# Graph attention and a GCN layer: transposing x1's rows in square blocks by VectorE and DMA, with three more products in the seven-product form

## The chip, the cores and the metric

One core of one Trainium2 chip runs the whole kernel. The metric is the device time of one execution in microseconds. Where a profile is quoted, PE is TensorE (PEld its weight loads), DVE is VectorE, ACT is ScalarE, POOL is GpSimd and SP is SyncE, which here only issues DMAs. L740 is line 740 of the kernel before.

## What is computed

All arrays are f32. x is 4096 x 512, adj is 4096 x 4096, the attention weights are 512 x 512, W1 is 512 x 128 and W2 is 128 x 512.

```python
q, k, v = x @ Wq.T + bq, x @ Wk.T + bk, x @ Wv.T + bv
a = q @ k.T / sqrt(512) + adj + adj
x1 = layernorm(x + softmax(a) @ v)
h = relu(adj @ (x1 @ W1) + b1)
out = layernorm(x1 + adj @ (h @ W2) + b2)
```

## The kernel before, in words

Rows are handled in 8 groups g of 512 (each of 4 row blocks r of 128). The scores are not made from q and k. The kernel forms M from Wq and Wk (`psm`, L856), then for each group u = M^T x^T (`psu`), and scores come from x^T and u alone; the softmax weights multiply x itself (`p`, L576), and only then comes the product with Wv.

Most large products use a seven-product form (Winograd's variant of Strassen's): the two operands are cut into quarters, seven half-size products are made instead of eight, and sums and differences of quarters go to other engines. `OPERANDS` names the operands of each product and `ORDER` their order. S1 to S4 are sums of quarters of the left operand (`form_s`), T1 to T4 of the right one. A transposing product by the identity matrix is used where a tile must be turned.

**Stages.** Time is cut into units of 7 steps; 16 units make a stage. In stage g, each step holds two products of the scores of group g (`qk`, L436), and beside them come items of a work list: the products `p` of group g-1 with x, and, at the start of the stage, the rows of group g-2 (`row_items`, L754). Items have a cost in microseconds; the loop at the end pops them at an even rate over the stage, so their order in the list is the order on every engine. `between(n)`, written `w(n)` in the list, takes n items of `p`; an item of cost 0 issues no matmul. So the rows of groups 0 to 5 lie in stages 2 to 7; those of group 6 lie beside `p` of group 7 in a stage 8 that has no scores, and those of group 7 beside the first product of the second layer. Stage 0 has no rows; its list holds the products of u for later groups.

**The rows of a group** (`row_items`): the product with Wv, for groups 0 to 5 (`FAST_V`) in the seven-product form (`rows_out_fast`, L659, 28 matmuls of 128x256), for groups 6 and 7 in the plain one (`rows_out`, L645, 16 matmuls of 128x512); the layer norm (`norm`: `rows_norm`, L726, on ACT); `add_b2` (L729), which adds b2 on POOL and stores the row block; `project` (L736), which turns a row block of x1 by four 128x128 transposes on PE (`x1ps`, L740) and copies them out by ACT into `x1t` (L742); and `project2` (L745), four matmuls of x1t with W1 (`tps`, L749). x1 stands in `xr`, one buffer, and x1t in one buffer that it shares with the scratch tile s3 of `rows_out_fast`.

**u.** Groups 0 and 1 use the plain form (`u_products`, L254, 16 matmuls of 128x512 each, L262); u of group 0 is computed before the first scores, and u of group 1 beside units 0 to 2. Groups 2 to 7 use the seven-product form (`u_fast`, L194, 28 matmuls of 128x256 each, L234) beside units 3 to 15. Its operands T1 to T4 of M come from `m_sums` and `m_t3`. u of groups 1 to 7 is stored to DRAM (`store_u`) and loaded back in its stage.

**DMA.** SP issues in program order the loads of x for `p` (`xn`, L506 and L510, three phases ahead; a phase is one operand of one block of 2 or 4 tile pairs), those of the score operands (`sa`, L342 and L347, five products ahead) and others. An instruction that waits holds up all that SP has behind it. ACT stores the score constants of a group by `store_c` (`c_d`, L417): 512 separate values of 4 bytes to DRAM.

Of the kernel before, what the change touches and what calls it, by code (L numbers as in the profile page):

```python
# [18 lines left out]
P = 128  # L19
# [5 lines left out]
def tile_graph_attention_then_gcn(  # L25
# [79 lines left out]

    c_d = [dram.tile([1, W], F32, name=f"c_d{g}") for g in range(NG)]
    u_d = [dram.tile([P, 7, 2, HW], F32, name=f"u_d{g}") for g in range(NG)]
    s_d = {
# [44 lines left out]

    FAST_V = range(NG - 2)
    QUARTER = {1: (0, 0), 2: (0, 0), 6: (1, 0), 7: (1, 1), 5: (1, 1), 4: (1, 0), 3: (0, 1)}
# [9 lines left out]
    def new_uo(b, what):  # L165

        u = UO.setdefault(b, {})
        if what in (B11, B12):
            u[what] = uop.tile([P, 2, HW], F32, tag="b1", name=f"b1_{b}_{what}", bufs=3)
        else:  # L170
            u["all"] = uop.tile([P, 5, 2, HW], F32, tag="ut", name=f"uo{b}")
            u.update({k: u["all"][:, k - 1] for k in range(1, 6)})

    def store_u(b, what):
        if what in (B11, T4):
            nc.gpsimd.dma_start(u_d[b][:, what], UO[b][what])
        else:
            nc.gpsimd.dma_start(u_d[b][:, 1:6], UO[b]["all"])

    def m_sums():  # L180

        m = m_t.rearrange("p (f c) (h o) -> p f h c o", f=2, h=2)
        for k, v in ((B11, m[:, 0, 0]), (T3, m[:, 0, 1]), (B21, m[:, 1, 0]), (B22, m[:, 1, 1])):
            MV[k] = v
        MV[T1] = t_sb[:, 28:32, :].rearrange("p (c a) b -> p c (a b)", c=2)
        MV[T2], MV[T4] = (ms_t[:, n] for n in range(2))
        for out_, a, b_ in ((T1, T3, B11), (T2, B22, T1), (T4, B21, T2)):
            nc.gpsimd.tensor_tensor(MV[out_], MV[a], MV[b_], ALU.subtract)

    def m_t3():  # L190

        nc.vector.tensor_tensor(MV[T3], MV[B22], MV[T3], ALU.subtract)

    def u_fast(b):  # L194
# [4 lines left out]
        def read(k):  # L199
            ps = X["X" if k in (1, 6, 5, 3) else "Y"].rearrange("p (o i) -> p o i", o=2)  # L200
            if k == 1:
                new_uo(b, B11)
            if k == 6:
                new_uo(b, B12)
            if k == 7:
                new_uo(b, "all")
            to = UO[b][{1: B11, 2: B11, 6: B12, 4: B12, 7: B22, 5: B22, 3: B21}[k]]
# [9 lines left out]
            if k == 4:  # L217
                for out_, a, b_ in ((T1, B12, B11), (T2, B22, T1), (T3, B22, B12)):
                    nc.gpsimd.tensor_tensor(u[out_], u[a], u[b_], ALU.subtract)
                store_u(b, B11)  # L220
            if k == 3:
                store_u(b, "all")
                owing.append(lambda: last(b))

        def last(b):
            nc.vector.tensor_tensor(UO[b][T4], UO[b][B21], UO[b][T2], ALU.subtract)
            store_u(b, T4)

# [23 lines left out]
        return [one(k, j) for k in ORDER for j in range(2)]  # L252

    def u_products(b):  # L254

        ps = {}

        def one(o, c):
            def go():
                if c == 0:  # L260
                    ps[o] = bank("o", f"psu{b}_{o}", 4)
                nc.tensor.matmul(  # L262
                    ps[o], m_t[:, c, ts(o, P)], XTS[b][:, c, :], start=c == 0, stop=c == ND - 1
                )
                if c == ND - 1:
                    if o == 0:
                        if b:
                            for what in (B11, B12, "all"):
                                new_uo(b, what)
                        else:  # L270
                            for k in ORDER:
                                new_operand(0, k)
                    pair = (B11, B12) if o < 2 else (B21, B22)
                    for h in range(2):
                        nc.scalar.activation(
                            (UO[b][pair[h]] if b else UT[0, pair[h]])[:, o % 2, :],
                            ps[o][:, ts(h, HW)],
                            AF.Identity,
                            bias=ub_t[:, o : o + 1],
                            scale=HALF_SCALE,  # L280
                        )
                    if o == ND - 1:
                        if b:
                            combine_u(nc.gpsimd, UO[b])
                            for what in (B11, "all", T4):
                                store_u(b, what)
                        else:
                            combine_u(nc.vector, {k: UT[0, k] for k in range(7)})

            return go  # L290

        return [one(o, c) for o in range(ND) for c in range(ND)]

    def combine_u(eng, ut):
        for out_, a, b_ in ((T1, B12, B11), (T2, B22, T1), (T3, B22, B12), (T4, B21, T2)):
            eng.tensor_tensor(ut[out_], ut[a], ut[b_], ALU.subtract)

# [361 lines left out]
    def rows_out_fast(g, k, j):  # L659
# [5 lines left out]
        tt = nc.vector.tensor_tensor  # L665

        def read(k):
            ps = T["VX" if k in (1, 6, 5, 3) else "VY"].rearrange("p (j o) -> p j o", j=2)
            h, i = QUARTER[k]
            to = XR[g][:, 2 * h : 2 * h + 2, ts(i, HW)]  # L670
            tt(to, ps, to, ALU.add)
# [18 lines left out]
        if (k, j) == (1, 0):  # L690
            read_px()
            T["s3"] = rowp.tile([P, 2, HW], F32, tag="x1t", name=f"s3_{g}")
            tt(T["s3"], a11, a21, ALU.subtract)
            tt(a21, a21, a22, ALU.add)
        if j == 0 and k in (1, 2, 7):
# [16 lines left out]
        if j == 0 and n:  # L712
            read(ORDER[n - 1])
            if k == 2:
                tt(a11, a21, a11, ALU.subtract)
            if k == 6:
                tt(a12, a12, a11, ALU.subtract)
            if k == 3:
                stats(2)
# [16 lines left out]
    def project(g, r):  # L736
# [5 lines left out]
        nc.scalar.copy(x1t.rearrange("p c i -> p (c i)"), ps)  # L742
        T["x1t", g, r] = x1t

    def project2(g, r):  # L745
# [8 lines left out]
    def row_items(g, between):  # L754
# [3 lines left out]
        def item(us, f, *args):  # L758
            return us, lambda: f(*args)
# [15 lines left out]

        w = between
        if g in FAST_V:
            return [
                *(item(0.86, rows_out_fast, g, k, j) for k in ORDER for j in range(2)),
                *w(1), item(0, rows_last, g), *norm(2), *norm(3), *w(2), *pro(2), *w(2), *pro(3),  # L780
                *w(1), *norm(0), *w(1), *pro2(2), *norm(1), *w(2), *pro(0), *w(2), *pro2(3), *w(2),
# [11 lines left out]
    with tc.tile_pool(name="wqk", bufs=1) as wp:  # L793
# [46 lines left out]

        for w_t, w_n, name, b_t, b_r in (
            (wq_t, wq_n, "bk", bk_t, bk_r), (wk_t, wk_n, "bq", bq_t, bq_r)
        ):
            in_every_row(name, b_t, b_r)
            for o in range(ND):
                ps = bank("o", f"psw{o}", 4)
                for c in range(ND):
                    nc.tensor.transpose(ps[:, ts(c, P)], w_t[:, c, ts(o, P)], ident)
                evict(o, w_n[:, o, :], ps)
        times(wq_t, bk_r, g_c)  # L850
        times(wk_t, bq_r, ub_t)

        for a in range(ND):
            ps = bank("o", f"psm{a}", 4)
            for o in range(ND):
                nc.tensor.matmul(  # L856
                    ps, wq_n[:, o, ts(a, P)], wk_n[:, o, :], start=o == 0, stop=o == ND - 1
                )
            evict(a, m_t[:, a, :], ps)
            if a == 1:  # L860
                in_every_row("g", g_c, g_t)
                times(bq_r.unsqueeze(1), bk_r, c0_t)
                for r in range(PER):
                    row_parts(r, rows0[:, r, :])
                add_c0(0)

    SLOTS = 12

    adjp = ctx.enter_context(tc.tile_pool(name="adjp", bufs=SLOTS))
    first = u_products(0)  # L870
    for f in first[:ND]:
        f()
    row_consts(0)
    begin_scores(0, 0)
    add_scores(0, 0)
    for f in form_s(0):
        f()
    for f in first[ND:]:
        f()

# [15 lines left out]

    work = {}
    work[0] = 3, [(0.86, f) for f in u_products(1)]
    work[3] = 13, [(0.86, f) for g in range(2, NG) for f in u_fast(g)] + [(0, lambda: owing.pop()())] * 2
    at(1, 0, m_sums)  # L900
    at(3, 0, m_t3)
    for g in range(2, NG):
# [216 lines left out]
    for g in range(NG):  # L1119
# [8 lines left out]
        for q in range(NP):  # L1128
            d, j = divmod(q, 2)
            if (g or d) and j == 0:  # L1130
                early = 2 + (g == 1 and d < 2)
                at(s0 + q - early, 4, begin_scores, g, d)
                at(s0 + q - early, 5, add_scores, g, d)
            for h in range(2):
# [262 lines left out]
```

## Time and profile before

| | |
|---|---|
| median of 3 runs | 2304.07 us (2303.71 to 2310.33) |
| profiled execution, its own time | 2308.84 us |
| its span in the trace | 2307.1 us |
| granted TensorE clock, mean | 0.998 |
| PE busy | 2276.3 us, 99% |
| DVE busy | 1617.0 us, 70% |
| POOL busy | 1018.7 us, 44% |
| ACT busy | 399.8 us, 17% |
| DMA queue q1 (SP), share of 16 engines | 52.3% |
| DMA queue q0 (POOL), share of 16 engines | 20.7% |

The span is the time from the first to the last instruction in the trace. Matmuls are pipelined, so what one costs is read from the distance between the starts of neighbours. An f32 matmul stands as two records in the trace, a transpose as one.

### The profile page before, as it was taken

What the parts mean: (1) busy time and instruction counts of PE and PEld (TensorE: products, weight loads), DVE (VectorE), ACT (ScalarE), POOL (GpSimd) and SP (SyncE); (2) the same over time, 40 slices, a digit from 0 to 9 for tenths busy, and PEclk for the clock granted to TensorE, in tenths of its full rate; (3) what the DMA queues carried; (4) which work ended last, traced back from release to release, by engine and by line L of the source; (5) the groups of instructions that cost most, each with busy time, mean ns of one, the idle gap of its engine ahead of it and who ended that gap; (6) DMA issues with size and microseconds to landing.
All of it is one profiled execution on the core that took longest, in us unless ns stands there. A gap on an engine that the chain in (4) does not pass through costs nothing.

```text
span 2307.1 us, 28475 instructions
## 1 busy us (share of the span) xinstructions
PE 2276.3 (99%) x10672; PEld 1750.6 (76%) x10672; DVE 1617.0 (70%) x2276; ACT 399.8 (17%) x438; POOL 1018.7 (44%) x1009
## 2 busy tenths in 40 slices
PE   9999999999999999999999999999999999999998
PEld 5888788888888888888888888888876743333456
DVE  4676776687667756765776687568657877888864
ACT  2212211131122112111311121122102000000012
POOL 3565654185327424731653274237429830001043
PEclk9999999999999999999999999999999999999999
DMA  6999878667857684777578586947754468899996
GB/s 177 273 284 309 233 215 230 193 174 215 246 135 218 189 246 114 215 213 215 151 221 232 145 218 193 259 117 210 196 191 155 155 237 321 332 347 375 352 383 218
DMA packets 282711, 525.14 MB, mean 228 GB/s; under 512 B 23184, under 2 KB 130448, under 8 KB 281680
## 3 DMA queue, kind: packets, MB, share of 16 engines
q1 hardware_dynamic: 229040, 406.12, 52.3%
q0 software_dynamic: 43296, 105.39, 20.7%
q10 hardware_dynamic: 10240, 11.82, 1.7%
q8 instruction: 85, 1.39, 0.2%
q14 instruction: 50, 0.41, 0.0%
HBM read 475.27 MB, written 46.41 MB: 226 GB/s over the span
## 4 chain that ended last, share of the span: by engine, by line
PE 92%; DVE 4%; POOL 2%; DMA 1%; issue 1%; ACT 0%; SPq 0%; POOLq 0%; DVEq 0%; ACTq 0%
PE p L576 32%; PE X L436 18%; PE b L1041 15%; PE Y L436 14%; PE v L703 3%; PE acce L1342 2%; PE psu L234 2%; PE ops L1296 1%; PE tps L749 1%; PE psu L262 1%; PE x L651 1%; PE x1ps L740 1%; DVE s L449 1%; PE psm L856 1%; DMA u_d<-uo 1%
## 5 line engine op out<-in xcount | busy, mean ns | idle before, releaser
L576 PE MATMUL p<-s,xn 128*128 128x256 f32 x3584 | 895.6, 380 | 7.0 <-DVE s L531 2.6
L576 PEld LDWEIGHTS p<-s,xn 128*128 128x128 f32 x3584 | 677.1, 190 | 111.0 <-DVE s L531 5.6
L436 PE MATMUL X<-ut,sa 128*128 128x256 f32 x1984 | 513.4, 381 | 1.7 <-DVE s L449 1.7
L492 POOL TENSOR_TENSOR lacc<-lacc,s 128x512 f32<-128x512 f32 x240 | 344.1, 1434 | 203.2 <-ACT s L483 192.3
L436 PEld LDWEIGHTS X<-ut,sa 128*128 128x128 f32 x1984 | 370.1, 190 | 64.2 <-DVE s L449 15.3
L449 DVE TENSOR_TENSOR s<-X,s 128x512 f32<-128x512 f32 x256 | 176.3, 689 | 278.6 <-PE X L436 278.2
L436 PE MATMUL Y<-ut,sa 128*128 128x256 f32 x1408 | 361.6, 380 | 0.2 <-DVE s L449 0.2
L436 PEld LDWEIGHTS Y<-ut,sa 128*128 128x128 f32 x1408 | 266.8, 190 | 37.7 <-issue 1.4
L483 ACT ACTIVATE s<-s 128x1024 f32<-128x1024 f32 x128 | 135.3, 1057 | 790.3 <-DVE s L479 790.3
L458 DVE TENSOR_TENSOR macc<-macc,s 128x512 f32<-128x512 f32 x240 | 258.1, 1075 | 1.2
L449 DVE TENSOR_TENSOR s<-Y,s 128x512 f32<-128x512 f32 x192 | 131.9, 687 | 157.0 <-PE Y L436 155.7
L479 DVE TENSOR_TENSOR s<-s,mb 128x512 f32<-128x512 f32 x256 | 231.2, 913 | 2.4 <-ACT mb L399 2.4
L385 POOL DMA_DIRECT2D s<-in_adjT_dram x64 | 84.4, 1318 | 256.7 <-ACT s L380 255.9
L549 DVE TENSOR_TENSOR ot<-p,ot 128x512 f32<-128x512 f32 x248 | 168.9, 681 | 31.4 <-PE p L576 31.2
L1008 DVE TENSOR_TENSOR tt<-ck 128x1024 f32<-128x1024 f32 x112 | 138.4, 1270 | 38.7 <-PE b L1041 33.6
L1041 PE MATMUL b<-tt,st 128*64 128x512 f32 (+1 forms) x768 | 156.0, 541 | 0.0
L380 ACT COPY s<-cb 128x2048 f32<-128x2048 f32 x64 | 121.0, 1890 | 48.1 <-PE p L576 39.8
L519 POOL TENSOR_TENSOR s<-s 128x256 f32<-128x256 f32 x128 | 124.6, 974 | 0.6
L1041 PEld LDWEIGHTS b<-tt,st 128*64 128x64 f32 x768 | 53.9, 137 | 87.8 <-issue 79.9
L526 DVE TENSOR_TENSOR s<-s 128x512 f32<-128x512 f32 x128 | 114.3, 914 | 0.0
L520 POOL TENSOR_TENSOR s<-s 128x256 f32<-128x256 f32 x128 | 107.8, 842 | 10.0
L489 POOL TENSOR_TENSOR lacc<-s 128x512 f32<-128x512 f32 x8 | 10.6, 1321 | 197.9 <-ACT s L483 197.9
(186 smaller groups left out, 2112.6 us busy)
## 6 DMA issues: line engine op xcount, KB each, us to landing
ck<-in_adjT_dram SPq DMA_DIRECT2D x128, 1024.0 KB, 7.4
s<-in_adjT_dram POOLq DMA_DIRECT2D x64, 1024.0 KB, 11.5
sa<-s_d SPq DMA_DIRECT2D x224, 256.0 KB, 5.7
xn<-in_x_dram SPq DMA_DIRECT2D x192, 256.0 KB, 4.3
xn<-xs_d SPq DMA_DIRECT2D x96, 512.0 KB, 5.7
sa<-in_xT_dram SPq DMA_DIRECT2D x168, 256.0 KB, 4.7
xn<-xs_d SPq DMA_DIRECT2D x64, 256.0 KB, 3.9
ut<-u_d SPq DMA_DIRECT2D x49, 256.0 KB, 7.2
```

The costliest lines, as they stand in the source:

```text
L380: nc.scalar.copy(s, CB[g].unsqueeze(1).to_broadcast([P, 4, W]))
L436: nc.tensor.matmul(T["X" if k in (1, 6, 5, 3) else "Y"][:, ts(j, HW)], SA[g, d, a][:, c, j, :], UT[g, b][:, c, :], start=k in (1, 2, 7) an ...
L449: nc.vector.tensor_tensor(ck, ps, ck, ALU.add)
L458: nc.vector.tensor_tensor(MACC[g], MACC[g], ck[:, h, :], ALU.max)
L479: nc.vector.tensor_tensor(ck, ck, MB[g], ALU.subtract)
L483: nc.scalar.activation(ck, ck, AF.Exp, scale=2.0)
L492: nc.gpsimd.tensor_tensor(LACC[g], LACC[g], ck[:, h, :], ALU.add)
L519: nc.gpsimd.tensor_tensor(b12, b12, b11, ALU.subtract)
L549: nc.vector.tensor_tensor(to, ps, to, ALU.add)
L576: nc.tensor.matmul(T["PX" if k in (1, 6, 5, 3) else "PY"][:, ts(f, HW)], XN[n][:, q - a, ts(f, P)], quarters(g, q)[{1: 0, 2: 2, 6: 1, 7: 0 ...
L1008: nc.vector.tensor_tensor(t[:, :2], v[:, :, 1], v[:, 0], ALU.subtract)
L1041: nc.tensor.matmul(BK[n][k][ts(half, HH)], lhs, right(u, i, half, b), start=q == 0, stop=q == NP - 1,)
```

## The change

1. `project` is replaced for groups 0 to 5 by three steps. `turn_blocks` lets VectorE transpose each 32x32 block of a row block [128, 512] within its place in the grid of blocks (one instruction). `store_blocks` writes the result to DRAM by four DMAs from SP, each of 32 partitions, in runs of 32 values (128 bytes), so that the blocks come to their transposed places. `load_blocks` loads it back (256 KB) over the row block in `xr`, and `project2` multiplies from there. `row_items` has a new order for these groups.
2. Group 6 also takes the seven-product form for Wv; its four sums of operands go to POOL.
3. u of groups 0 and 1 also takes the seven-product form. The start of the kernel is rearranged: the last two transposes of Wk come between the first products of M, the operands of u are formed there, and u of group 0 precedes the first scores. u of groups 1 to 7 is spread over units 1 to 15.
4. The small u tiles get a ring of four buffers in place of three and take one tile (B21) from the large one, which is stored earlier; B21 is stored by ACT. The initial scores for tiles 2 and 3 of group 0 (d = 1) are begun four places earlier.

```diff
@@ const
+    xt_d = {
+        (g, r): dram.tile([P, ND, P], F32, name=f"xt_d{g}_{r}")
+        for g in range(NG - 2)
+        for r in range(PER)
+    }
-    FAST_V = range(NG - 2)
+    FAST_V = range(NG - 1)
@@ new_uo, store_u
-        if what in (B11, B12):
-            u[what] = uop.tile([P, 2, HW], F32, tag="b1", name=f"b1_{b}_{what}", bufs=3)
+        if what in (B11, B12, B21):
+            u[what] = uop.tile([P, 2, HW], F32, tag="b1", name=f"b1_{b}_{what}", bufs=4)
...
-        if what in (B11, T4):
+        if what == B21:
+            nc.scalar.dma_start(u_d[b][:, what], UO[b][what])
+        elif what in (B11, T4):
...
-            nc.gpsimd.dma_start(u_d[b][:, 1:6], UO[b]["all"])
+            nc.gpsimd.dma_start(u_d[b][:, 2:6], UO[b]["all"])
@@ m_sums
+            for eng, out_, a, b_ in (
+                (nc.gpsimd, T1, T3, B11), (nc.vector, T2, B22, T1), (nc.vector, T3, B22, T3),
+                (nc.gpsimd, T4, B21, T2),
+            )
@@ rows_out_fast
+        sum_ = (nc.gpsimd if g == NG - 2 else nc.vector).tensor_tensor
...
-            tt(T["s3"], a11, a21, ALU.subtract)
-            tt(a21, a21, a22, ALU.add)
+            sum_(T["s3"], a11, a21, ALU.subtract)
+            sum_(a21, a21, a22, ALU.add)
...
-                tt(a11, a21, a11, ALU.subtract)
+                sum_(a11, a21, a11, ALU.subtract)
...
-                tt(a12, a12, a11, ALU.subtract)
+                sum_(a12, a12, a11, ALU.subtract)
@@ after project
+    def turn_blocks(g, r):
+        T["x1t", g, r] = rowp.tile([P, ND, P], F32, tag="x1t", name=f"x1t{g}_{r}")
+        nc.vector.transpose(T["x1t", g, r].rearrange("p c i -> p (c i)"), XR[g][:, r, :])
+
+    def store_blocks(g, r):
+        x1t = T.pop(("x1t", g, r))
+        to = xt_d[g, r].rearrange("(b i) c (a j) -> a i c b j", i=32, j=32)
+        for a in range(4):
+            nc.sync.dma_start(
+                to[a], x1t[ts(a, 32)].rearrange("i c (b j) -> i c b j", j=32)
+            )
+
+    def load_blocks(g, r):
+        T["x1t", g, r] = XR[g][:, r, :].rearrange("p (c i) -> p c i", i=P)
+        nc.sync.dma_start(T["x1t", g, r], xt_d[g, r])
@@ row_items
+        if g < NG - 2:
...
+            return [
+                *(item(0.86, rows_out_fast, g, k, j) for k in ORDER for j in range(2)),
+                *w(1), item(0, rows_last, g), *norm(2), *norm(3), *w(8), *norm(0), *w(2), *norm(1), *w(3),
+                *b2(2), *w(3), *turn(2), *w(5), *store(2), *b2(3), *w(11), *turn(3), *load(2), *w(5),
+                *store(3), *b2(0), *w(11), *turn(0), *load(3), *pro2(2), *w(5), *store(0), *b2(1),
+                *w(11), *turn(1), *load(0), *pro2(3), *w(5), *store(1), *w(11), *load(1), *pro2(0),
+                *w(14), *pro2(1),
+            ]
@@ work list of stage 0
-    work[0] = 3, [(0.86, f) for f in u_products(1)]
-    work[3] = 13, [(0.86, f) for g in range(2, NG) for f in u_fast(g)] + [(0, lambda: owing.pop()())] * 2
-    at(1, 0, m_sums)
-    at(3, 0, m_t3)
+    work[1] = 15, [(0.86, f) for g in range(1, NG) for f in u_fast(g)] + [(0, lambda: owing.pop()())] * 2
```

## The prediction

> **What bounds the kernel now.** I read the page's busy times first, then the granted clock (0.998, so no throttling to win back), then busy time by stage, then who PE waits for.
>
> ```profile
> PE 2276.3 (99%) x10672; PEld 1750.6 (76%) x10672; DVE 1617.0 (70%) x2276; ACT 399.8 (17%) x438; POOL 1018.7 (44%) x1009
> ```
>
> ```profile
> 870.00:1084.00 214.00, 213.63 (x1014) 186.66 (x1013) 145.49 (x210) 42.24 (x42) 98.98 (x91) 1.00 0.70 197
> ```
>
> The second line is one stage with rows (columns: window and length, then busy time and count of PE, PEld, DVE, ACT, POOL, then clock, DMA share, GB/s). PE is never free: 213.63 of 214 us. DVE has 68 us spare, DMA engines 30%. So in stages 2 to 7 PE work taken away is time gained, as long as nothing new makes PE wait. The list of PE's waits from 300 to 1700 us has a single line:
>
> ```profile
> PE x1ps L740 <- ACT xr L639: 2.3, 6, 0.4
> ```
>
> That is the first transpose of each of six groups waiting for its norm. The transposes themselves, in the timeline of PE:
>
> ```profile
> 678.03 1.03 PE L436 MATMUL Y<-ut,sa 128*128 128x256 f32 x4
> 679.43 0.66 PE L740 MATMUL x1ps<-ident,xr 128*128 128x128 f32 x4 [0.37 <-ACT xr L639]
> 679.92 0.60 PE L576 MATMUL p<-s,xn 128*128 128x256 f32 x2
> ...
> 681.65 0.60 PE L740 MATMUL x1ps<-ident,xr 128*128 128x128 f32 x4
> 682.09 1.03 PE L436 MATMUL X<-ut,sa 128*128 128x256 f32 x4
> ```
>
> From start to start a group of four costs 682.09 - 681.65 = 0.44 us. In the same way eight records of 128x256 take 1.73 us (chain, L703), so 0.43 a matmul, and 24 records of 128x512 take 10.30 us (chain, L262), so 0.86 a matmul.
>
> **Part 1, transposes off PE.** Removed: 6 groups x 4 x 0.44 = 10.6 us, and the 2.3 us of waits above: 12.9 us, all on the path. ACT loses 24 copies of 0.59 us, which were never waited for beyond these.
>
> Added on DVE: 24 transposes of 128x512. The trace has no such instruction. From below: nothing, if it fills idle time; the nearest row is any 128x512 f32 pass on DVE, 0.69 us (L449). I take 0.69, so 4 x 0.69 = 2.8 us in a stage with 68 us spare: no cost. If that cover were gone it would be 16.6 us in all. The Trainium skill ("VectorE: DVE Perf Modes", The three transpose paths) gives 311 ns for 128x128 in bf16 and recommends TensorE for a full 128x128; four times that is an estimate of 1.24 us, 30 us in all, still inside the spare time.
>
> Added on SP: per row block four stores and one load, so 5 x 24 = 120 DMAs. A 256 KB issue holds SP for 0.3 to 0.9 us in the timeline, so a store is out 1.5 to 3 us after it begins. What waits behind them is the open question. In SP's queue stand the `xn` and `sa` loads. On DVE, the transposes of the second, third and fourth row block wait until the previous store has landed, because x1t is one buffer; 3 x 6 = 18 such waits, with everything DVE does for PE behind them. On PE, project2 waits for the load.
>
> The cover: a stage's list is 14 x 0.86 + 224 x 0.43 + 4 x 0.9 = 112 us over 112 steps, 1.0 us a step, and a step lasts 0.86 (scores) + 1.0, about 1.9 us. 11 items of p are 4.7 steps, 9.0 us, between a store and the next transpose; 5 items are 4.1 us between a transpose and its store; 14 to 16 items are 11.5 to 13 us from a load to its project2. DVE may be late by some 3 us more: a bank of scores is written again one product (3.8 us) after its last, of which the read takes 0.69. So **a store may land up to 12 us after it begins**.
>
> When does it land? It is 2048 runs of 128 bytes. From below: 256 KB stored in 2 KB runs (`x_d`) lands in 4.0 us (median, table of DMA issues); with the four issues, 6 to 7 us. From above: the only small stores are those of `c_d`, 512 runs of 4 bytes.
>
> ```profile
> q1 hardware_dynamic: 101, 0.11, 11.3%
> q10 hardware_dynamic: 528, 0.00, 2.8%
> xn<-in_x_dram SPq DMA_DIRECT2D x2, 256.0 KB, 12.0
> sa<-in_xT_dram SPq DMA_DIRECT2D x2, 256.0 KB, 12.5
> xn<-xs_d SPq DMA_DIRECT2D x1, 512.0 KB, 10.5
> sa<-s_d SPq DMA_DIRECT2D x1, 256.0 KB, 12.3
> c_d<-c_sb ACTq DMA_DIRECT2D x1, 2.0 KB, 11.4
> ```
>
> These are the DMAs of the 9 us after one such store (window 329.46 to 338.46). Its packets took 2.8% of 16 engines, 4.0 us / 528 = 7.6 ns each, yet it landed after 11.4 us, and loads that take 4.3 us on the page's median took 12. Small writes can thus hold up all DMA by some 7 us per 512 runs; four DMAs in a row would be 29 us. Against that: sixteen of the 4-byte values share 64 bytes, while the 128-byte runs are 32 times larger and far apart, so I take them to be nearer to ordinary packets: between 7.6 ns for 4 bytes and q1's 52.3% x 16 x 2307.1 us / 229040 = 84 ns for a mean of 1773 bytes, a straight line gives 13 ns, 2048 x 13 ns / 16 = 1.7 us. Landing then is 8 to 9 us after the store begins: just inside the 9.0, and within the 12.
>
> The Trainium skill ("DMA: Bandwidth & Descriptors", Specifications) speaks against this change: below 512 bytes a DMA engine does read-modify-write. Counting each run as 512 bytes makes 1 MB, which its table of measured times has at 6.15 us; by that estimate landing would be 10 to 11 us, so DVE waits and PE does not. If read-modify-write serializes as the `c_d` row may show, the sum turns to a loss.
>
> I allow 3 us for PE: 18 waits at 0.17, half the 0.37 that PE now waits for a norm; bounds 0 and the rivals below. The remaining order (norms of rows 0 and 1 later, b2 earlier) stays beside p at no cost: PE no longer asks for these rows before project2. b2's `sa` buffers are asked for 16 items apart in place of 4.
>
> **Part 2, group 6.** 16 x 0.86 = 13.8 becomes 28 x 0.43 = 12.0, and the 0.9 us wait of L651 for DVE goes: -2.6. The four sums on POOL take 1.27 each (its 128x512 row at 1725.94); POOL is idle until 1724, the products begin at 1718.1. The first three are done 1.3 + 1.3 + 1.3 after read_px, about 1723; the third product wants the last of them at 1718.1 + 3.4 + 0.4: a wait of 1 us. Net -1.6, bounds 0 (the next thing late in this stage is POOL's lacc or DVE's subtraction, both in the chain) and -3.
>
> **Part 3, u and the start.** u of groups 0 and 1: 2 x (16 x 0.86 - 28 x 0.43) = -3.4. The 0.5 us wait for wk_t is filled by products of M. M's last sums (DVE 0.69 twice, POOL 1.27) lie behind the first two products of u (3.4 us) and the next three. The last read of u (ACT 0.84) lies behind the first product of scores. If that cover fails: 1 us. **Part 4:** PE's one wait in stage 0 for `uo` (1.9 us, with `u_d<-uo` at 13.6 us in the chain) goes, as the large tile is stored earlier. Together -5.8; bounds -2 and -6.
>
> **Sum.** -12.9 + 3 - 1.6 - 5.8 = -17.3 us, against the profiled execution (2308.84, of which the span is all but 1.7). That execution lies 4.8 above the median; the difference is applied to the median: 2304.07 - 17.3 = **2287**. Without the allowance and with every bound at its best, 2304 - 12.9 - 3 - 6 = 2282, some margin below: 2277.
>
> **Rivals.**
> - *Store too slow, slower than before.* Store landing beyond 12 us stops DVE in place of PE's transposes: 18 x (landing - 12). It eats the gain at 12 + 17/18, about 13 us. With the latest landing of `c_d` in the trace, 15.6 us, it is 18 x 3.6 = 65: 2287 + 65 = 2352; at 29 us, 2287 + 306 = 2593. For: the `c_d` row. Against: the runs' size and spread. Chance 0.18.
> - *Stores land, but loads behind them come late.* In the blocks of 2 pairs, three phases of 4 items are 12 x 0.43 x 1.9 = 9.8 us ahead, the load takes 4.3, so 5.5 spare. If a store delays it as `c_d` did (7.7), PE waits 2.2 us at the two stores in such blocks: 12 x 2.2 = 26, 2313; with half that delay none; the middle is about 12 us: 2299, not to be told from no change. For: SP is one queue in order. Against: no `xn` wait on PE from 300 to 1700 although c_d's bursts lie there. Chance 0.12.
> - *More than forecast*, below 2277: if DVE and DMA also lose waits. Nothing shows it: 0.04.
> - *The transposes leave PE and PE doesn't end sooner*, because DVE is what sets the stage: excluded by its 68 spare us but for the last stage. Within the range.
>
> **Numbers.** Forecast 0.66, range alone 2277 to 2296. The rivals 0.18, 0.12 and 0.04. Taking in the second rival, 2277 to 2306 holds 0.78. A measurement tells 0.3%, 6.9 us, from no change: faster (below 2297) 0.66 + 0.04 + a quarter of the second rival, 0.73; same 0.09; slower 0.18.
>
> **What would show it.** Right: no L740 records of groups 0 to 5; stages of 212 us in place of 214.4; store landing under 10 us; DVE's transposes near 0.69; PE's list of waits from 300 to 1700 short. Wrong: DVE idle before its transposes on the stores, project2 waiting for DMA, `xn` landings well over 4.3 us, or a first score later than 38 us (now 39.5).

## The result, and the profile after

The changed kernel takes **2325.66 us** (median of 4 runs, 2322.13 to 2329.61) where the kernel before takes 2305.07 beside it (4 runs, 2303.71 to 2310.33): a ratio of 1.0086, 95% interval 1.0073 to 1.0099. It is slower by 20.6 us; 2287 was forecast. The profiled execution of the changed kernel took 2324.45 us, with a span of 2322.7 and a mean granted clock of 0.998. That of the kernel before (2308.84) lies 3.8 us above its median, this one 1.2 below, so the two spans differ by 15.6 us and not by 20.6.

Busy time on the page of the changed kernel, to set beside the first line shown above:

```profile
PE 2266.0 (98%) x10648; PEld 1752.1 (75%) x10648; DVE 1641.9 (71%) x2311; ACT 388.5 (17%) x418; POOL 1027.0 (44%) x1007
```

PE did lose work (10.3 us of busy time in all), and the span grew by 15.6 us all the same. So PE now stands idle. One stage of the changed kernel, from the start of one row product (the product with Wv) to the next, in the columns of the stage shown above (window, length, PE, PEld, DVE, ACT, POOL, clock, DMA share, GB/s):

```profile
870.70:1088.50 217.80, 212.87 (x997) 184.63 (x996) 151.90 (x213) 39.77 (x37) 100.76 (x91) 1.00 0.76 203
```

A stage was 214.2 us, 212 was forecast, and it is 217.8: PE is idle for 4.9 us of it. DVE is idle for 66 us and POOL for 117 us; by these averages nothing but PE could set the end. The list of PE's waits from 300 to 1700 us says otherwise. It had one line before (`x1ps`, 2.3 us); of the changed kernel it is:

```profile
PE p L549 <- DVE ot L522: 19.0, 12, 1.7
PE p L549 <- DVE s L499: 6.4, 11, 0.8
PE p L549 <- DVE s L504: 3.8, 6, 0.6
```

(Columns: total us, times, longest.) L549 is the product of the softmax weights with x (L576 before), L522 the read of its accumulator, L499 and L504 two of the passes (`px_t34`, `px_t1`) that make the T operands out of the weights. None is a part of the change, none is a DMA, and none is behind the new transposes. The three sum to 29.2 us, 4.9 a stage. The account of the span: the first row product starts 4.7 us earlier (435.1 for 439.8), the stages from there to the row product of group 6 take 21.0 us more, the rest 0.7 less: +15.6.

What the prediction feared is fine. The DMA issues of the changed kernel from 300 to 1700 us (count, KB each, median us to landing):

```profile
xt_d<-x1t SPq DMA_DIRECT2D x96, 64.0 KB, 5.1
xr<-xt_d SPq DMA_DIRECT2D x24, 256.0 KB, 6.2
```

DVE never waits for a store, and PE never for a load of x1.

### The profile page after: what moved, and what is told of

Read it like the earlier page. It is cut to its first block, busy times and chain, and to the rows that moved or that the text cites. A ratio compares the mean times of both kernels' runs of the same rounds, so it can differ in the third digit from the quotient of the medians.

```text
span 2322.7 us, 28686 instructions
## 1 busy us (share of the span) xinstructions
PE 2266.0 (98%) x10648; PEld 1752.1 (75%) x10648; DVE 1641.9 (71%) x2311; ACT 388.5 (17%) x418; POOL 1027.0 (44%) x1007
## 4 chain that ended last, share of the span: by engine, by line
PE 88%; DVE 8%; DMA 2%; issue 1%; POOL 1%; ACT 0%; SPq 0%; POOLq 0%; DVEq 0%
PE p L549 29%; PE X L409 18%; PE b L1060 15%; PE Y L409 13%; PE v L678 3%; PE psu L251 3%; PE acce L1362 2%; DVE s L452 2%; DVE s L499 1%; DVE s L504 1%; PE tps L742 1%; PE ops L1316 1%; DMA t_sb<-in_x_dram 1%; DVE s L422 1%; DVE ot L522 1%
## 5 line engine op out<-in xcount | busy, mean ns | idle before, releaser
L549 PE MATMUL p<-s,xn 128*128 128x256 f32 x3584 | 898.3, 381 | 35.8 <-DVE ot L522 19.8
L549 PEld LDWEIGHTS p<-s,xn 128*128 128x128 f32 x3584 | 675.6, 190 | 147.1 <-DVE ot L522 26.2
L465 POOL TENSOR_TENSOR lacc<-lacc,s 128x512 f32<-128x512 f32 x240 | 345.7, 1440 | 183.6 <-ACT s L456 172.8
L422 DVE TENSOR_TENSOR s<-X,s 128x512 f32<-128x512 f32 x256 | 176.3, 689 | 275.5 <-PE X L409 272.5
L422 DVE TENSOR_TENSOR s<-Y,s 128x512 f32<-128x512 f32 x192 | 131.9, 687 | 185.3 <-PE Y L409 185.2
L452 DVE TENSOR_TENSOR s<-s,mb 128x512 f32<-128x512 f32 x256 | 237.2, 932 | 0.7 <-ACT mb L372 0.7
L431 DVE TENSOR_TENSOR macc<-macc,s 128x512 f32<-128x512 f32 x240 | 234.5, 977 | 1.4
L522 DVE TENSOR_TENSOR ot<-p,ot 128x512 f32<-128x512 f32 x248 | 168.8, 681 | 23.9 <-PE p L549 23.7
L499 DVE TENSOR_TENSOR s<-s 128x512 f32<-128x512 f32 x128 | 126.9, 1011 | 0.0
L492 POOL TENSOR_TENSOR s<-s 128x256 f32<-128x256 f32 x128 | 125.7, 982 | 0.6
L493 POOL TENSOR_TENSOR s<-s 128x256 f32<-128x256 f32 x128 | 116.7, 911 | 10.0
L462 POOL TENSOR_TENSOR lacc<-s 128x512 f32<-128x512 f32 x8 | 10.6, 1325 | 198.0 <-ACT s L456 198.0
```

The costliest lines, as they stand in the source:

```text
L422: nc.vector.tensor_tensor(ck, ps, ck, ALU.add)
L431: nc.vector.tensor_tensor(MACC[g], MACC[g], ck[:, h, :], ALU.max)
L452: nc.vector.tensor_tensor(ck, ck, MB[g], ALU.subtract)
L465: nc.gpsimd.tensor_tensor(LACC[g], LACC[g], ck[:, h, :], ALU.add)
L492: nc.gpsimd.tensor_tensor(b12, b12, b11, ALU.subtract)
L499: nc.vector.tensor_tensor(b, b, t2, ALU.subtract)
```

## Where in the stage

PE's timeline in one of the stages of the changed kernel, 57 us after its start (us of start, duration; in brackets the idle time before it and what ended that):

```profile
927.38 1.13 PE L549 MATMUL p<-s,xn 128*128 128x256 f32 x4 [0.30 <-DVE s L499]
...
930.18 1.13 PE L549 MATMUL p<-s,xn 128*128 128x256 f32 x4 [0.81 <-DVE s L499]
...
933.92 1.13 PE L549 MATMUL p<-s,xn 128*128 128x256 f32 x4 [1.75 <-DVE ot L522]
...
938.21 0.70 PE L549 MATMUL p<-s,xn 128*128 128x256 f32 x2 [1.43 <-DVE ot L522]
```

DVE's timeline of the same time:

```profile
930.92 1.75 DVE L452 TENSOR_TENSOR s<-s,mb 128x512 f32<-128x512 f32 x1
932.60 0.68 DVE L422 TENSOR_TENSOR s<-X,s 128x512 f32<-128x512 f32 x1
933.20 0.67 DVE L522 TENSOR_TENSOR ot<-p,ot 128x512 f32<-128x512 f32 x1
933.79 0.41 DVE L504 TENSOR_TENSOR s<-s 128x256 f32<-128x256 f32 x1
934.13 1.75 DVE L452 TENSOR_TENSOR s<-s,mb 128x512 f32<-128x512 f32 x1
935.80 1.75 DVE L431 TENSOR_TENSOR macc<-macc,s 128x512 f32<-128x512 f32 x1
937.48 0.68 DVE L522 TENSOR_TENSOR ot<-p,ot 128x512 f32<-128x512 f32 x1
```

There is no idle bracket: DVE runs without a pause, so the read L522 that PE waits for begins only at 933.2 and 937.5, behind passes that were queued before it. And two lengths stand side by side for tiles of one shape. L422 and L522 take one operand from PSUM (`X`, `p`) and one from SBUF: 0.68 us. L452 (the shift by the row maxima, `mb`) and L431 take both from SBUF: 1.75 us. POOL's timeline tells what lies beside them:

```profile
930.67 1.45 POOL L707 TENSOR_TENSOR xb<-xr,b_t 128x512 f32<-128x512 f32 x1
932.42 0.60 POOL L709 DMA_DIRECT2D x_d<-xb  x1 [0.30 <-POOL xb L707]
933.85 3.15 POOL L465 TENSOR_TENSOR lacc<-lacc,s 128x512 f32<-128x512 f32 x2 [0.84 <-ACT s L456]
936.97 1.17 POOL L492 TENSOR_TENSOR s<-s 128x256 f32<-128x256 f32 x1
```

The three passes of 1.75 us lie beside POOL's additions (L707, L465), and so does the read L522 of 937.48 (beside L492), which keeps its 0.68. It is so all over the stages: from 300 to 1720 us, the 206 passes of L452 and L431 that meet no work of POOL take 0.67 to 0.69 us, the 155 that share more than 0.4 us with a computing pass of POOL take 0.64 to 2.98, and the 208 passes of L422 and L522 that share as much take 0.67 to 0.69.

The windows of 15 us make it a burst and not a state (columns as above; the third lies late in the stage):

```profile
900.70:915.70 15.00, 14.36 (x66) 11.92 (x65) 13.34 (x16) 3.52 (x5) 14.11 (x15) 1.00 0.85 194
915.70:930.70 15.00, 13.89 (x63) 11.61 (x62) 13.06 (x16) 4.39 (x4) 14.36 (x13) 1.00 0.90 226
990.70:1005.70 15.00, 15.00 (x70) 12.97 (x69) 6.15 (x11) 2.77 (x2) 2.69 (x3) 1.00 0.86 243
```

DVE 13.3 and POOL 14.1 of 15 us early, 6.2 and 2.7 late. In the kernel before, the window that answers to the second, the fullest of the three from 30 to 75 us:

```profile
913.25:928.25 15.00, 15.00 (x75) 13.32 (x74) 12.12 (x16) 6.03 (x6) 12.64 (x11) 1.00 0.59 145
```

**Theories.** Theory 1, the first I formed: the list now has 5.36 us less of PE items ahead of the early `p` (4 x 0.44 for the transposes, 4 x 0.9 for `project2`, which stands later), so `p` runs some five steps ahead of the passes that feed it, and it is the pace of the list that does it. Rivals: the new DVE transposes and the order on DVE (theory 2 in the first expectations, later D); the new DMAs (3, later M); `add_b2` earlier on POOL (4); parts 2 to 4. Theory 4 finds no support in the lists: from 900 to 945 us the kernel before has four of these passes and the changed kernel three. **Theory P**, formed after e1, e2, e3 and e5, when theory 1 no longer held: between 30 and 75 us of a stage DVE and POOL need nearly all the time, since a DVE pass with two SBUF operands is stretched from 0.68 to 1.75 us beside a POOL pass. In the kernel before, PE's own transposes and `project2` lay just there and covered it. This time is called the burst from here on.

## The experiments

Times of kernels with one run are of one execution; the kernel before took 2304.66 to 2305.43 (medians) beside them. "Waits" are PE's from 300 to 1720 us.

**e1_parts_2_to_4**: the change without part 1.

```diff
-        if g < NG - 2:
+        if False:
             turn, store, load = (
```

> Part 1 undone: all groups turn x1 on PE in the old order; group 6's products, u and the start stay changed. All theories that put the loss into stages 2 to 7 (pace of p, DVE transposes, DMA, b2) agree: stages back to 214.2 us each, the 4.7 us gained before the first row product kept, so about 2300 us, faster than before by 4 to 6 us. If it is instead near 2325, the loss is not in part 1 at all.

Measured 2305.9 (2302.38 to 2309.25, 10 runs), ratio 1.0002, 0.9992 to 1.0012; stages of 214.0 to 214.5 us, and no wait for DVE in them. So the 20 us are part 1's alone, and parts 2 to 4, from which 7.4 were expected, give nothing that can be measured. In the traces the same scores stand 5.1 us earlier at 231 us than in the trace of the kernel before, and the first row product 0.9 us earlier. But 3.4 of the 5.1 are that one execution's: in e11 below, whose program is the kernel before up to there, the same scores already come 3.4 us earlier. So the gain by 231 us is about 1.8 us, and part of it goes again at the end of stage 0, where the DMA engines are full. Windows of this kernel:

```profile
225.00:235.00 10.00, 8.89 (x42) 6.94 (x41) 7.41 (x10) 0.84 (x2) 8.88 (x10) 1.00 1.09 317
235.00:245.00 10.00, 7.23 (x29) 5.82 (x27) 4.56 (x7) 1.68 (x3) 2.71 (x3) 0.83 1.05 385
```

The DMA share is 1.05 to 1.09, PE is busy 16.1 of 20 us, and its longest wait between 200 and 300 us is 2.8 us for a load of score operands (`sa`); in the changed kernel that wait is 1.2.

**e2_pace**: the order and pace of the list as before, by empty items that only charge their cost.

```diff
+            idle = lambda us: [item(us, lambda: None)]
+            late2 = lambda r: [item(0, project2, g, r)]
...
-                *w(1), item(0, rows_last, g), *norm(2), *norm(3), *w(8), *norm(0), *w(2), *norm(1), *w(3),
+                *w(1), item(0, rows_last, g), *norm(2), *norm(3), *w(2), *idle(0.44), *w(2), *idle(0.44),
+                *w(2), *idle(0.9), *w(2), *norm(0), *idle(0.44), *w(2), *norm(1), *idle(0.9), *w(2),
...
```

> All of the change kept, but 5.36 us of empty items are charged early in the list, where project and project2 stood before, and project2 is charged at nothing, so that p advances over the steps exactly as it did before. Theory 1 (p runs 5 steps ahead, and its sums on DVE and POOL fall into the unit with two tile pairs of the softmax): PE's 4.9 us of waits for DVE in each of six stages go, about 2304 - 17 = 2287, between 2283 and 2295. Theory 2 (24 transposes more on DVE), theory 3 (stores and loads) and theory 4 (b2 earlier on POOL; it stands at the same items here, so 1 to 2 us later only) expect most of the waits to stay: 2310 to 2325.

Measured 2322.84 (2319.63 to 2326.09, 4 runs), ratio 1.008, 1.0065 to 1.0095, waits 25 us (of another mix: 8.3 of them for the scores, 3.6 for loads of x). By the costs in the list `p` is spread over the steps as before, and nothing is won. Theory 1 falls. The reason is argued and not measured: a step without its PE work is shorter, so DVE and POOL have no more time in it.

**e3_pe_turns_same_pace**: the changed list, but PE turns the row blocks at the places of the DVE transposes; no store, no load.

```diff
+            turn = lambda r: [item(0, project, g, r)]
...
```

> The row order and pace of the changed kernel, but x1 turned by PE and ACT as before, at the place where VectorE's transpose stood; no store, no load, project2 a few items earlier. Theory 1: the waits of PE for DVE stay, at most a third smaller for want of the transposes, and 10.6 us of PE work come back: 2320 to 2335. Theories 2 and 3: no waits, 2325.7 - 29 + 10.6, about 2300 to 2308.

Measured 2331.73 (1 run), stages of 218.6 us. PE has all its work of before again, without the new DMAs and DVE transposes, and the loss is no smaller: its place in the stage matters. The waits are 17.0 us, more than a third below 29, and a lower clock takes part of that back: 0.92 and 0.86 in two windows of 7.5 us beside the wait, an estimate of 1.7 us a stage. The time lay in the range of theory 1, which this run alone could not reject.

**e5_no_dma**: DVE transposes kept, no store and no load: `project2` reads `x1t`, whose blocks are turned but stand in their old places, so x1 W1 has other values. The edit takes the `store` and `load` items out of the list, and `project2` comes a few items earlier.

> The row order and pace of the changed kernel, with VectorE's transposes, but no store and no load: project2 multiplies x1t as VectorE leaves it, with the 32x32 blocks in their old places, so x1 @ W1 and all behind it have other values. Theory 3 (DMA holds up DVE, POOL or the loads): no waits, about 2287 to 2295. Theories 1, 2 and 4: the 4.9 us of waits in each stage stay within 1 us, 2318 to 2326.

Measured 2323.1 (1 run). The time lies in the range of theories 1, 2 and 4, but the waits are 19.6 us, 3.3 a stage and not within 1 of 4.9. The clock was at half for 17 us between 300 and 1720, an estimate of 8.5 us, which the changed kernel did not lose there. So this run alone doesn't show that the DMAs and the place of `project2` are free.

**e4_no_dve_turns**: the stores read `xr` itself and the DVE transposes are left out (x1 W1 has other values).

```diff
-        T["x1t", g, r] = rowp.tile([P, ND, P], F32, tag="x1t", name=f"x1t{g}_{r}")
-        nc.vector.transpose(T["x1t", g, r].rearrange("p c i -> p (c i)"), XR[g][:, r, :])
+        T["x1t", g, r] = XR[g][:, r, :].rearrange("p (c i) -> p c i", i=P)
```

> The changed kernel without VectorE's transposes: the stores read the row block itself, so the blocks come to their places unturned and all behind x1 @ W1 has other values; the DMAs and the order stay. Theory P: the transposes are 2.1 of some 38 us of DVE in the burst, the waits fall from 29 us to 15 to 25, time 2312 to 2322. Theory D: waits below 8, time 2290 to 2300. Theory M: no change, 2322 to 2328.

Measured 2327.89 (1 run), with 28.3 us of waits. The DVE transposes cost nothing that shows. Theory P had expected a share of the loss from them, and that share fails. By its time this run fits theory M. In e6 and e9 every DMA stays and the loss of 20 us is gone, so the DMAs alone don't cost it.

**e6_no_row_sums**: the changed kernel without 30 of the 31 POOL passes of each group that add up the softmax denominators (240 of L465; the denominators have other values). The expectations of e10 and e11 say 31 of 32.

```diff
-            for h in range(2):
-                nc.gpsimd.tensor_tensor(LACC[g], LACC[g], ck[:, h, :], ALU.add)
+            pass
```

> The changed kernel without POOL's sums of the softmax rows (only the first pair of tiles of each group is summed), so 240 POOL passes of 1.44 us are left out and the output has other values; DVE, DMA, PE and the order stay. Theory P (DVE and POOL together have no time left between 30 and 75 us of a stage, because a DVE pass with two SBUF inputs takes 1.75 us in place of 0.68 beside a POOL pass, and the PE work taken away was their cover): PE's 29 us of waits from 300 to 1720 us fall below 6, time about 2285 to 2296. Theory D (the 24 transposes and the order on DVE alone) and theory M (stores and loads): waits stay above 20, time above 2315.

Measured 2287.89 (1 run), waits 7.2 us, a little over the 6 expected. Less work on POOL, which is idle for half of the stage, makes PE end 36.6 us sooner. DVE's list of this kernel from 900 to 945 us, against the changed kernel's, has the reason (count, busy us, mean ns):

```profile
L452 DVE TENSOR_TENSOR s<-s,mb 128x512 f32<-128x512 f32 x11 | 8.0, 730 | 0.0
...
L422 DVE TENSOR_TENSOR s<-X,s 128x512 f32<-128x512 f32 x7 | 4.8, 692 | 9.3 <-PE X L409 9.3
```

And the changed kernel:

```profile
L452 DVE TENSOR_TENSOR s<-s,mb 128x512 f32<-128x512 f32 x9 | 13.1, 1459 | 0.0
...
L422 DVE TENSOR_TENSOR s<-X,s 128x512 f32<-128x512 f32 x6 | 4.1, 687 | 3.1 <-PE X L409 3.0
```

The shift falls from 1459 to 730 ns although nothing of DVE was touched; the pass with an operand in PSUM has 0.69 us in both. (The other pass with two SBUF operands, L431, falls from 1177 to 1039 only: part of POOL's other work still lies beside it.)

**e8_pe_filler**: the changed kernel with PE work that does nothing (transposes of the identity, 12 x 0.45 us a stage) where the kernel before had its transposes and projections.

```diff
+            def cover(n):
+                for m in range(n):
+                    ps = mbank(f"cover{g}_{m}")
+                    for c in range(ND):
+                        nc.tensor.transpose(ps[:, ts(c, P)], ident, ident)
...
```

> The changed kernel with empty PE work put back: 12 groups of four transposes of the identity (0.45 us each, read by nobody) in each of the six stages where project and project2 stood before, 32 us of PE work in all. Theory P: this work falls into time in which PE waits anyhow; waits fall to under 10 us in all and the time stays within 8 us of the changed kernel, 2318 to 2334. Theories D and M: 32 us longer, 2350 to 2358.

Measured 2334.68 (1 run), 0.7 us beyond theory P's range; waits 14 us where under 10 were expected, of which 2.5 for DVE's passes of the burst and scores and 3.7 of the added work itself for DVE. 32 us of added PE work cost some 9 us. Of the 23 that don't show, the lists of waits account for 15 (29.2 to 14.1): that much of the added work lies in time in which PE waited anyway. This is the cover, seen from the other side; the other 8 have no line.

**e7_rows_late**: the rows' chain behind the norms begins only after 62 items of `p`, beyond the burst.

```diff
-                *w(1), item(0, rows_last, g), *norm(2), *norm(3), *w(8), *norm(0), *w(2), *norm(1), *w(3),
-                *b2(2), *w(3), *turn(2), *w(5), *store(2), *b2(3), *w(11), *turn(3), *load(2), *w(5),
+                *w(1), item(0, rows_last, g), *norm(2), *norm(3), *w(8), *norm(0), *w(2), *norm(1), *w(51),
+                *b2(2), *turn(2), *w(5), *store(2), *b2(3), *w(11), *turn(3), *load(2), *w(5),
```

> The changed kernel with b2, the transposes, stores, loads and project2 of a group begun 62 items of p into the stage in place of 14 to 17, behind the burst. Theory P: POOL loses four passes of 1.5 us and their DMA issues, DVE three transposes in the burst; PE's waits fall from 4.9 us a stage to 1 to 3, time 2295 to 2312. Theory D: waits of some 4 us move with the transposes or stay: 2318 to 2326. Theory M: the same as D, at the later place.

Measured 2338.27 (2326.27 to 2343.46, 4 runs), ratio 1.0129, 1.009 to 1.0168: a miss. The waits of the burst fell to 13.9 us, but another came. SP's and DVE's lines of its timeline:

```profile
992.24 7.00 SPq L730 DMA_DIRECT2D xt_d<-x1t  x4
...
1003.47 0.71 DVE L724 STREAM_TRANSPOSE x1t<-xr 128x512 f32<-128x512 f32 x1 [7.93 <-DMA xt_d<-x1t]
```

The issue of four stores took 7.0 us, so the next DVE transpose waited 7.9 us for `x1t`, and PE behind it 5.4 us for its scores. After the wait the clock was low, too (0.66 from 1000 to 1010 us). This is the prediction's first rival, the store that stops DVE, in a kernel that puts the stores later, where DMA is full (share 1.04 from 1000 to 1004). In the changed kernel it does not occur.

**e9_after_max_in_psum**: the changed kernel, but the maxima stay in PSUM (groups 0 to 6). The row product takes its accumulators from the ring of four to free the bank.

```diff
-        MB[g] = bcp.tile([P, W], F32, tag="mb", name=f"mb{g}")
-        in_every_row(f"m{g}", T.pop(("m", g)), MB[g])
...
+        m_tags[:] = ["m1"]
+        MB[g] = bank("m0", f"mb{g}")
+        m = T.pop(("m", g))
+        for r in range(PER):
+            nc.tensor.transpose(MB[g][:, ts(r, P)], m[:, r : r + 1].to_broadcast([P, P]), ident)
...
-            T["VX" if k == 1 else "VY"] = mbank(f"v{g}_{k}")
+            T["VX" if k == 1 else "VY"] = bank("o", f"v{g}_{k}", 4)
```

> The changed kernel, with one thing altered in stages 1 to 7: the broadcast row maxima that the shift reads stay in their PSUM bank and are not copied to SBUF, so a shift has one operand in SBUF and one in PSUM; for the bank, the row product's two accumulators come out of the ring of four. The work and its order are the same, but for the ScalarE copy of the maxima. Theory P (VectorE and GpSimd are what ends last between 30 and 75 us of a stage, since a VectorE pass with two SBUF operands takes 1.75 us beside a GpSimd pass and 0.68 us alone): the 9 shifts of 900 to 945 fall from a mean of 1.46 us to under 0.9, the 29 us that PE waited for VectorE in 300 to 1720 fall under 12, and the time to 2290 to 2308. Rival (the steps of p are bound by GpSimd alone, VectorE's length is only a by-product): shifts shorter, waits and time within 5 us of the changed kernel, 2320 to 2330. Rival (the order of PE's own work costs it, whatever the other engines do): 2320 to 2330 as well, with PE's waits gone.

Measured 2306.53 (2302.17 to 2309.53, 10 runs), ratio to the kernel before 1.0004, 0.9994 to 1.0013. POOL adds what it added, DVE makes the same passes, and one operand of one of them stands in another memory: 19 of the 20 us are gone. (ScalarE's copy of the maxima and the banks of the row product differ as well; neither was tried by itself.) The shift in the list of this kernel from 900 to 945 us, and PE's waits from 300 to 1720:

```profile
L460 DVE TENSOR_TENSOR s<-s,mb 128x512 f32<-128x512 f32 x11 | 7.4, 676 | 0.0
```

```profile
PE p L557 <- DVE s L512: 5.7, 6, 1.0
PE p L557 <- issue: 3.3, 6, 0.6
PE v L682 <- POOL ot L694: 1.3, 1, 1.3
```

676 ns where it had 1459; the waits are 10.3 us where they had 29. The rival that POOL alone binds the steps falls, as POOL's passes are as long as they were (1447 ns for 1488).

**e10_after_no_row_sums_2** and **e11_before_no_row_sums**: the edit of e6, on the changed kernel and on the kernel before, measured together.

> The changed kernel without the row sums that GpSimd adds up (31 of 32 passes a stage are left out, so its divisors are wrong), as before, now to be set beside its counterpart in the same call: 2285 to 2291.

> The kernel before without the same row sums (31 of 32 GpSimd passes a stage left out, wrong divisors). Theory P: in the kernel before the 24 transposes and their project2 products hid GpSimd and VectorE, and PE waited for them 2.7 us in 300 to 1720, so there is nothing to gain: 2300 to 2306. Then the change, which costs 20 us with the row sums, saves 12 to 18 us without them, near the 17.3 of the prediction. If the changed rows list costs time by itself, this kernel falls as far as the changed one did, to 2265 to 2275, and the change costs 20 us here too.

Measured, side by side: 2285.52 (2284.23 to 2287.48, 4 runs) for the changed kernel, ratio 0.9913, 0.9898 to 0.9928, and 2302.56 (2299.74 to 2307.39, 10 runs) for the kernel before, ratio 0.9989, 0.9979 to 0.9999. The same 30 passes a group are worth 40 us to the one and 2.4 to the other. **Without them the change saves 17.0 us**, with them it costs 20. That 17.0 is close to the 17.3 forecast is luck in part: of the 13.7 us between the spans of these two profiles, 11.3 come from five stages (212.4 to 213.7 us against 214.5 to 215.6) and 0.7 from the start, for which 5.8 were forecast.

**e12_max_in_psum_bias_late**: e9, and the four bias additions on POOL (`add_b2`), with the loads and `project2` that follow them, moved behind the burst; turns and stores keep their places.

```diff
...
-                *b2(2), *w(3), *turn(2), *w(5), *store(2), *b2(3), *w(11), *turn(3), *load(2), *w(5),
+                *turn(2), *w(5), *store(2), *w(11), *turn(3), *w(5), *store(3), *w(11), *turn(0), *w(5),
+                *store(0), *w(11), *turn(1), *w(5), *store(1), *w(25),
+                *b2(2), *load(2), *w(8), *b2(3), *load(3), *w(8), *b2(0), *load(0), *w(8), *b2(1),
...
```

> The kernel with the maxima in PSUM, and with one more thing taken out of 30 to 75 us of a stage: GpSimd's four bias additions (1.4 us each), with the loads and project2 products that must follow them, stand after the last p product of that time; turns and stores stay where they are. Theory P: the 10.3 us that PE still waits in 300 to 1720 fall under 6 and the time to 2295 to 2303, a little under the kernel before. If what is left of the waits there comes from VectorE passes of its own list (the T sums beside the row sums), nothing moves: 2304 to 2308. If the later loads meet the loads of x, as in the kernel with the rows late, PE waits for DMA or for VectorE's transposes and the time is over 2310.

Measured 2303.13 (2301.09 to 2308.12, 11 runs), ratio 0.9991, 0.9982 to 1.0001. The time lies between the two ranges, 0.1 us above that of theory P. Waits 9.4 us, not under 6: those for the T operands fell from 5.7 to 2.3, and 2.5 came for the scores. Stages are 213.85 us, 0.4 less than e9's. It is the fastest kernel here that computes everything, but not measurably faster than the one before.

## Why the prediction was wrong

**The step that failed** is the first one: "DVE has 68 us spare ... So in stages 2 to 7 PE work taken away is time gained, as long as nothing new makes PE wait." Nothing new does make PE wait. What makes it wait was there before, covered by the work that the change removes. The 68 us are an average over 214 us. Between 30 and 75 us of the stage (898.25 to 943.25) DVE was busy for 34.8 of 45 us and POOL for 35.0, in the window of 913 us above for 12.1 and 12.6 of 15; in the changed kernel the same stretch holds 39.0 and 40.3. The 5.36 us of PE work that the kernel before had there was the cover: 1.76 of transposes, which the change takes out of the stage, and 3.6 of `project2`, which it moves to later places. PE's waits in the changed kernel are 4.9 us a stage. That it takes both, the stretched passes and the PE work taken away, is what e10 and e11 show: without POOL's row sums the same change saves 17.0 us. The rival "DVE is what sets the stage" was "excluded by its 68 spare us": the rival that held, thrown out by the same average.

**Part 1 by its terms.** Removed from PE: right by the records (96 fewer than in e1, which are 24 groups of four). PE's busy time fell by 7.3 us from e1's, where 10.6 were summed from starts. DVE transposes "0.69, no cost": right. Their row in the changed kernel:

```profile
L724 DVE STREAM_TRANSPOSE x1t<-xr 128x512 f32<-128x512 f32 x3 | 2.1, 698 | 0.0
```

The estimate of 1.24 us from the Trainium skill's bf16 figure ("VectorE: DVE Perf Modes", The three transpose paths) is not what this f32 form takes. Store landing "8 to 9 us" after it begins: right by the medians; four issues of 0.63 us and a landing of 5.1 make some 7.6. At 925.06 four issues took 4.3 us, the latest landing of all is 11.7, and still DVE waited for none. The 10 to 11 us worked out from the Trainium skill's read-modify-write rule ("DMA: Bandwidth & Descriptors", Specifications) and a time that the page has for loads is not what the medians show. Loads of x land in 5.0 us where they took 4.3; no wait follows. The allowance of 3 us for PE: 29.2. In total part 1 costs 20 us where -9.9 was forecast (the changed kernel's +20.6 against e1's +0.5).

**Parts 2 to 4**, -7.4 forecast, +0.5 measured by e1 (interval -1.8 to +2.8). PE's records are as worked out (72 more in e1, in matmuls of half the width), and the first scores of the changed kernel come at 37.09 us for 39.52. Three terms failed. The wait for `uo`, 1.9 us in the sum, belongs to the one profiled execution: in e11's it is 0.5. It goes, but a longer one comes in its place in stage 0 of the changed kernel:

```profile
152.97 1.21 PE L409 MATMUL X<-ut,xt 128*128 128x256 f32 x4 [3.10 <-DVE s L422]
```

The read it waits for stands behind two DVE passes with a length of 1.74 and 1.76 us (L302, L301) among others, again beside passes of POOL, and from 153.9 the clock is at half for 3.4 us. The prediction named no such price, and none for the loads at the border of stages 0 and 1; which of these should yield wasn't tried. And the product of group 6 has waits of 0.67, 0.32 and 0.89 us where 0.9 was to go and 1 to come.

**The rivals.** The store that stops DVE did not come in the changed kernel; e7 shows that it is real where the stores stand later. Loads late: no wait in the list.

**Where it could have been seen.** The trace before had the price already. Its shifts from 900 to 945 us:

```profile
L479 DVE TENSOR_TENSOR s<-s,mb 128x512 f32<-128x512 f32 x12 | 12.8, 1077 | 0.0
```

They have a mean of 1077 ns, where L449, which reads one operand from PSUM, has 0.69 us. I read DVE's passes by that one row and took them to be of one length. The Trainium skill ("GPSIMD Engine Reference", Specifications) says that GpSimd shares its SBUF interfaces with VectorE and contends with VectorE instructions that have two SBUF inputs. The runs agree: 1459 ns beside the row sums, 730 without them, 676 with one operand in PSUM. The page has no price; here it is a factor of 2.6 at the median of the nine shifts (1.75 / 0.68), and the longest pass of L431 takes 2.98 us.

**What stays open.** e3's stages are 218.6 us, 6.6 over the 212 of a stage without transposes and waits: 1.8 are its transposes, 2.8 its waits, and of the other 2.0 the clock is an estimate of 1.7. The changed kernel's 217.8 are 5.8 over the 212, of which 4.9 are waits and 0.9 have no line. How much the new order of the rows costs by itself, apart from the PE work taken away, wasn't separated. How much of the burst could be spread by another order of the softmax passes wasn't tried.

## What to carry to other kernels

An engine's spare time counts only where the work taken away stood: read the busy time of the other engines in windows of some 15 us around that place, not over the stage, and treat work that is removed from the bounding engine as cover that somebody else may have used. Read the longest and the shortest duration of one form: where a pass of one shape has two lengths, look for what runs beside the longer. An operand that is only read, left in PSUM, can be worth more than the work saved elsewhere: here 19 us, where 12.9 were to be taken off PE.

## What was not expected of the hardware

- A VectorE addition over 128x512 f32 with both operands in SBUF takes 0.67 to 0.69 us where GpSimd does nothing, and 0.64 to 2.98 us where it shares more than 0.4 us with a GpSimd pass (median 1.2 for L452, 1.6 for L431). With one operand in PSUM it takes 0.67 to 0.69 us beside them too.
- The granted clock can fall after short waits. In e5 PE waits 2.63 us at 933.7 to 936.3; its windows (the last three columns are clock, DMA share, GB/s):

```profile
930.90:938.40 7.50, 4.80 (x20) 3.48 (x19) 7.32 (x10) 1.20 (x2) 6.30 (x6) 0.94 0.93 296
938.40:945.90 7.50, 7.50 (x34) 6.44 (x33) 3.19 (x6) 0.91 (x1) 6.06 (x6) 0.83 0.42 117
```

PE is busy all of the second window, at 0.83: inside it the clock is 0.50 from 937.5 to 940.8 and 1.00 from 941. After the waits of at most 1.75 us in the stages of the changed kernel the clock stayed at 1.00; in the 10 us of e7 that hold its wait of 5.4 us it was 0.66. The length alone doesn't decide: after the wait of 1.91 us for `uo` in the kernel before it was 0.50 from 144.9 to 148.2, after one of 2.38 us in e2 (until 151.93) it stayed at 1.00. The Trainium skill ("TensorE: Matmul & The Clock Gate", Part 1) gives an idle window of about 3.4 us as what halves the clock; here waits of 1.91 and 2.63 us were followed by half the clock. A wait of PE can thus cost more than its length.
- Stores of 512 runs of 128 bytes land in 5.1 us (median of 96), while one of 512 values of 4 bytes took 11.4 us in the kernel before.
